# Attention queries of 15 batches by seven block products instead of eight, in a graph network kernel

## Chip, core and metric

One core of a Trainium2 chip runs the whole kernel; everything is f32. The metric is the device time of one launch in microseconds. Engines: PE is TensorE (matrix products), DVE is VectorE, ACT is ScalarE, POOL is GpSimd, SP is SyncE, which issues the DMAs.

## The reference

Two layers work on x of 16 batches x 1024 nodes x 256 features. The first (graph aggregation, two dense layers with batch norms, residual, layer norm) is not touched by the change. The second is, per batch:

```
c_adj = mean(fea, axis=1)                       # fea = x transposed: 256 x 1024
A     = abs(abs(sigmoid(c_adj[n] - c_adj[m]) - 0.5) - 0.5) * 2
Wg    = adj * (A + A.T) / 2                     # gate, 1024 x 1024
g     = relu((fea @ Wg) * para)                 # queries, 256 x 1024
k, v  = split(x @ kv_w)
out   = softmax(q k^T * scale) v                # 4 heads of 64
x     = layernorm(x + out)
```

The product `fea @ Wg` is the one that the change does otherwise.

## The kernel before

The first layer runs until about 870 us of the span. It already does its large products by seven block products (`seven`, L104). The attention of all batches follows in `fast()` (L571), and there the order of all instructions is written out by hand: `tc.manual_schedule()` keeps the program order, and each engine works its queue in that order.

**Steps.** A batch is 16 steps. A step (L1188 to L1197) multiplies a block of keys with half a batch's queries for one pair of heads (`scores`, L780, matmul at L787, two PSUM buffers `ps_s`), takes the exponential (`exps`, L796, ACT at L799, six buffers `ep`), adds the exponentials up for the denominators (`sums`, L801, DVE at L805 and L808) and multiplies them with the values (`attend`, L815, PE at L823). Scores and exponentials run one step ahead. After four steps ACT copies one half of the output (L834) and DVE adds the other (L835).

**Pieces.** All other work of neighbouring batches is cut into pieces and put into slots, eight a batch (`put`, L961, from L967 on). Two slots of pieces are issued, then four steps: this is called a window here, four to a batch, numbered 0 to 3. `arrange` (L1052) orders the pieces of a slot. While batch b-1 has its steps, the pieces make batch b ready and begin batch b+1:

- `gate` (L723): ACT makes a 128x1024 block of the gate (`wg_a`, L705: L710, or L712 and L713), DVE finishes the block two before and multiplies it with adj (`wg_b`, L715: L719, L720). Eight blocks in slots 0 to 2 (`WG`, L964), each a tile of its own.
- `keys` (L731) and `values` (L741): PE at L736 and L747, copied out of PSUM by ACT; in slots 0 to 2 (`KV`).
- `graph` (L756): the product for the queries, 32 pieces of one matmul (L761), h over the two halves of the nodes, c over the two halves of the features, k over 8 blocks of 128 nodes, in slots 2 to 7 (`QG`). After each k = 7, `queries` (L767) multiplies with para (L769) and takes the relu with the scale (L770), both on DVE.
- `rows` (L616), `ln1_a` (L625) and `ln1_b` (L641): rows of batch b+1. DVE transposes and adds (L618, L619) and takes statistics (L562, L563), POOL makes scale and shift (L66, L68, L636), ACT normalises in place with a sum of each row (L646). `bn2_q` (L610) has scaled them before on POOL (L614).
- `put_x1`, `get_x1`, `x1_v` (L654 to L669): the transposed x by way of DRAM. `means` (L678) and `crow` (L683): the column means that the gate needs.
- `dens`, `fetch_o`, `finish_a`, `finish_b` (L846 to L925): denominators and the output's layer norm for the batch before.

All of these take PSUM tiles from `ps_t` (four buffers of one bank), and so does the output of `attend`, two tiles for four steps.

## Times and profile before

| | |
|---|---|
| median of 3 runs | 2460.53 us (2458.66 to 2460.64) |
| the profiled execution | 2461.81 us, its span 2460.1 us |
| granted PE clock | 0.993 |
| first score of the attention | 871.0 us into the span |
| one batch of attention, steady | 100.5 us |
| PE, DVE, ACT, POOL busy in such a batch | 100.4, 83.3, 59.0, 32.7 us |

The profiled execution is one run of its own; its span goes from the first instruction to the last. A row of a group reads: line, engine, operation, output<-inputs, shape, count, then busy time and mean ns of one, then idle time of the engine ahead of them and what ended it. A row of a timeline reads: start, duration, engine, line, operation, output<-inputs, count, and in brackets the idle time before and what ended it. In a table by stretches each engine has its busy time and its number of instructions. An f32 matmul appears as two records.

### The profile page before, as it was taken

Reading aid. Unit: us, or ns where it says so; the run is one execution under the profiler, and the core shown is the slowest. Engines: PE = TensorE matmul, PEld = TensorE weight load, DVE = VectorE, ACT = ScalarE, POOL = GpSimd, SP = SyncE. Lnnn points to the kernel's source line nnn. Section 1 sums busy time; section 2 is a strip of 40 time slices with the busy share of each in tenths; the row PEclk is TensorE's granted clock in tenths of the full one; section 3 lists DMA queues with packets and bytes.
Section 4 is the critical chain, followed back from the end, with each engine's and each line's share of the span. In section 5 each row is a group of like instructions: output and inputs, shape, how many; then the busy total and the mean of one; then the engine's idle time right before and its main releaser. Section 6 shows DMA issues by size and latency. Waiting matters only on the chain. (4 is left out here: it accounts for less than half of the span.)

```text
span 2460.1 us, 33873 instructions
## 1 busy us (share of the span) xinstructions
PE 2412.8 (98%) x12217; PEld 1009.9 (41%) x12217; DVE 1810.3 (74%) x2583; ACT 1094.1 (44%) x1549; POOL 777.2 (32%) x826
## 2 busy tenths in 40 slices
PE   8999999999899899999999999999999999999997
PEld 4444444444344443443434434344344343443432
DVE  5555545546766777888788888888888888888676
ACT  2000000001554455564655656656566465564644
POOL 2223222231566531414224143232342422414012
PEclk9999999999999999999999999999999999999998
DMA  4122122222578543544545535545364454554221
GB/s 137 68 86 103 69 86 103 82 87 88 192 278 277 133 121 84 142 122 114 141 105 124 148 89 149 120 119 148 82 150 111 119 147 96 139 128 110 68 42 52
DMA packets 583951, 292.73 MB, mean 119 GB/s; under 512 B 407528, under 2 KB 556512, under 8 KB 576608
## 3 DMA queue, kind: packets, MB, share of 16 engines
q1 hardware_dynamic: 583776, 290.49, 43.3%
q8 instruction: 98, 1.61, 0.3%
q14 instruction: 77, 0.63, 0.1%
HBM read 194.46 MB, written 95.94 MB: 118 GB/s over the span
## 5 line engine op out<-in xcount | busy, mean ns | idle before, releaser
L799 ACT ACTIVATE e<-s 128x1024 f32<-128x1024 f32 x512 | 495.8, 1020 | 327.8 <-PE s L787 264.7
L808 DVE TENSOR_TENSOR acc<-acc,e 128x1024 f32<-128x1024 f32 x384 | 508.5, 1324 | 113.3 <-ACT e L799 87.1
L787 PE MATMUL s<-qT,kT 64*64 64x512 f32 x4096 | 490.6, 594 | 4.5 <-ACT e L799 1.7
L823 PE MATMUL o<-e,v 64*64 64x512 f32 x4096 | 485.3, 589 | 0.0
L761 PE MATMUL pg<-wg,x 128*128 128x512 f32 x960 | 426.5, 597 | 0.0
L614 POOL TENSOR_TENSOR yt<-yt,stq 128x512 f32<-128x512 f32 x120 | 178.1, 1485 | 414.9 <-DMA yt<-yT 232.0
L761 PEld LDWEIGHTS pg<-wg,x 128*128 128x128 f32 x960 | 178.7, 190 | 238.6 <-issue 237.8
L823 PEld LDWEIGHTS o<-e,v 64*64 64x64 f32 x4096 | 156.6, 133 | 282.8 <-issue 275.1
L787 PEld LDWEIGHTS s<-qT,kT 64*64 64x64 f32 x4096 | 147.2, 133 | 298.4 <-issue 254.1
L107 ACT COPY u<-pa 128x512 f32<-128x512 f32 x15 | 8.8, 585 | 475.3 <-PE pa L312 475.3
L66 POOL TENSOR_SCALAR rs_z<-mv_z 128x2 f32<-128x2 f32 x64 | 18.2, 285 | 470.1 <-DVE mv_z L563 469.2
L720 DVE SCALAR_TENSOR_TENSOR wg<-wg,adj 128x1024 f32<-128x1024 f32 x128 | 163.4, 1308 | 2.8
L312 PE MATMUL pa<-AhT,x 128*128 128x512 f32 x360 | 161.8, 592 | 0.0
L646 ACT ACTIVATE x<-x,nm_a,rs_a 128x256 f32<-128x256 f32 x128 | 75.9, 594 | 171.5 <-POOL nm_a L636 171.1
L835 DVE TENSOR_TENSOR ot<-o,ot 128x512 f32<-128x512 f32 x64 | 44.2, 691 | 130.6 <-ACT ot L834 130.6
L747 PE MATMUL pv<-kvw,x1T 128*128 128x256 f32 x512 | 118.2, 384 | 0.0
L736 PE MATMUL pk<-x1T,kvw 128*128 128x512 f32 x256 | 117.9, 604 | 0.0
L343 PE MATMUL ph<-agg,SW 128*128 128x512 f32 x240 | 112.8, 592 | 0.0
L66 POOL TENSOR_SCALAR rs_a<-mv_a 128x2 f32<-128x2 f32 x64 | 38.0, 594 | 234.0 <-DVE mv_a L563 232.8
L747 PEld LDWEIGHTS pv<-kvw,x1T 128*128 128x128 f32 x512 | 96.7, 191 | 31.7 <-issue 16.2
L312 PE MATMUL pa<-T,sx 128*128 128x512 f32 x240 | 107.9, 592 | 0.0
L312 PEld LDWEIGHTS pa<-AhT,x 128*128 128x128 f32 x360 | 68.4, 190 | 86.1 <-issue 86.1
(193 smaller groups left out, 3155.2 us busy)
## 6 DMA issues: line engine op xcount, KB each, us to landing
adj<-in_adj_dram SPq DMA_DIRECT2D x128, 512.0 KB
h<-hT SPq DMA_DIRECT2D x28, 1024.0 KB
hL<-h SPq DMA_DIRECT2D x28, 1024.0 KB
ob<-o SPq DMA_DIRECT2D x248, 72.0 KB
x<-in_x_dram SPq DMA_DIRECT2D x16, 1024.0 KB
yT<-y SPq DMA_DIRECT2D x64, 256.0 KB
out_dram<-r SPq DMA_DIRECT2D x64, 256.0 KB
xr<-in_x_dram SPq DMA_DIRECT2D x62, 256.0 KB
```

The costliest lines, as they stand in the source:

```text
L312: nc.tensor.matmul(p, xs[n][:, k, :], bs[n][:, k, :], start=(k == 0), stop=(k == KN - 1))
L343: nc.tensor.matmul(p, ws[n][:, ts(f, P)], bs[n], start=True, stop=True)
L614: nc.gpsimd.tensor_tensor(y, y, sc, op)
L646: nc.scalar.activation(r, r, AF.Identity, bias=nm[:, a : a + 1], scale=rs[:, a : a + 1], accum_out=css[b][:, i : i + 1])
L720: nc.vector.scalar_tensor_tensor(t, t, 1.0, adjs[b * NT + i], op0=OP.add, op1=OP.mult)
L736: nc.tensor.matmul(p, kvw[:, k, ts(c, P)], x1Ts[b][:, k, ts(h, FB)], start=(k == 0), stop=(k == CT - 1))
L747: nc.tensor.matmul(p[:, ts(a, C)], x1Ts[b][:, k, ts(j + a, P)], kvw[:, k, C:], start=(k == 0), stop=(k == CT - 1),)
L761: nc.tensor.matmul(pg[b], x1s[b, k // 2][:, k % 2, ts(c, P)], wgs[b, k][:, ts(h, FB)], start=(k == 0), stop=(k == NT - 1))
L787: nc.tensor.matmul(t[r * HD : (r + 1) * HD, h, :], kTs[b, pair][h * HD : (h + 1) * HD, ts(2 * cb + r, HD)], qTs[b, pair, hf][h * HD : (h + ...
L799: nc.scalar.activation(E[g, a], S.pop((g, a)), AF.Exp)
L808: nc.vector.tensor_add(ACC[b, hf, pair], ACC[b, hf, pair], E[g, a])
L823: nc.tensor.matmul(O[b, hf, pair][r][h * HD : (h + 1) * HD, :], vs[b][r * HD : (r + 1) * HD, cb, pair * P + h * HD : pair * P + (h + 1) * HD],
```

## The change

It is made for batches 1 to 15, the pieces of which run during the 15 batches before; batch 0 keeps its eight products.

With x split into blocks x_ci (c half of the features, i half of the nodes) and the gate into b_ih, the four quarters of the product come from seven products of blocks, each 4 matmuls long. The sums of gate blocks are made in place, in `wgs` (one tile for the batch now), by four `sums_w` of 128x2048 on DVE; the sums of x blocks by `sums_x` on POOL, 10 instructions of 128x256, into a new tile. Products 1, 6, 7 and 4 are added onto each other in one PSUM bank (`ps_q`, taken from `ps_t`, which keeps three), which is copied by ACT after 1, 6 and 7; product 3 is added onto product 5 in another. `collect` makes the quarters on DVE: one reads PSUM alone and multiplies with para, three add PSUM to a copy first. The relu with the scale goes to ACT. The values' last two pieces move from slot 2 to slots 4 and 5, and x1T is allocated at the first `x1_v`.

```diff
-        wgp = pool("wgp", NT)
+        wgp = pool("wgp", 1)
...
-        qp = pool("qp", 2 * CT + 1)
+        qp = pool("qp", 2 * CT + 2)
+        sxp = pool("sxp", 1)
...
-        ps_t = pool("ps_t", 4, space=PSUM)
+        ps_t = pool("ps_t", 3, space=PSUM)
+        ps_q = pool("ps_q", 1, space=PSUM)
...
+        def sums_x(b, k):
+            if k == 0:
+                SX[b] = sxp.tile([P, 2, KN, P], F32, tag="sx", name=f"sx{b}")
+            for j in range(KN // 2):
+                p, q = (SX[b][:, n, 2 * j : 2 * j + 2, :] for n in range(2))
+                x00, x01, x10, x11 = (block_x(b, c, i, j) for c in range(2) for i in range(2))
+                if k == 0:
+                    nc.gpsimd.tensor_add(p, x10, x11)
+                    nc.gpsimd.tensor_sub(p, p, x00)
+                    nc.gpsimd.tensor_sub(q, x00, x10)
+                else:
+                    nc.gpsimd.tensor_add(q, x10, x11)
+                    nc.gpsimd.tensor_sub(p, x01, p)
+
+        def sums_w(b, n):
+            (b00, b01), (b10, b11) = ([block_w(b, i, h) for h in range(NH)] for i in range(2))
+            if n == 3:
+                nc.vector.tensor_sub(b01, b11, b01)
+            elif n == 2:
+                nc.vector.tensor_add(b00, b00, b01)
+            elif n == 4:
+                nc.vector.tensor_sub(b10, b10, b00)
+            else:
+                nc.vector.tensor_sub(b01, b11, b00)
...
+        def product(b, n):
+            c, i = {2: (0, 1), 4: (1, 1)}.get(n, (0, 0))
+            w = {1: (0, 0), 2: (1, 0), 3: (1, 1), 4: (1, 0), 5: (0, 1), 6: (0, 0), 7: (0, 1)}[n]
+            bank = {1: 0, 6: 0, 7: 0, 4: 0, 2: 1, 5: 2, 3: 2}[n]
+            if n in (1, 2, 5):
+                PB[b, bank] = (ps_t if bank else ps_q).tile([P, FB], F32, tag="t", name=f"pg{bank}")
+            for k in range(KN):
+                x_ = block_x(b, c, i, k // 2)[:, k % 2, :] if n in (1, 2, 4) else SX[b][:, n in (7, 5), k, :]
+                nc.tensor.matmul(
...
+                    start=(k == 0 and n in (1, 2, 5)),
+                    stop=(k == KN - 1),
...
+            if n == 1:
+                t = queries_tile(b, 0, 0)
+                queries_tile(b, 1, 0)
+                nc.scalar.copy(t, PB[b, 0])
+            if n in (6, 7):
+                nc.scalar.copy(queries_tile(b, n - 6, 1), PB[b, 0])
+
+        def collect(b, c, h):
+
+            t, p = qTs[b, c, h], PB[b, {(0, 0): 1, (1, 0): 0}.get((c, h), 2)]
+            if (c, h) != (1, 0):
+                nc.vector.tensor_add(t, p, t)
+                p = t
+            nc.vector.tensor_mul(t, p, para_sb[:, c, ts(h, FB)])
+
+        def relu(b, c, h):
+            nc.scalar.activation(qTs[b, c, h], qTs[b, c, h], AF.Relu, scale=scale)
...
-        KV = (2, 3, 3)
-        QG = (4, 6, 5, 5, 6, 6)
+        KV = (2, 3, 1)
...
+            for t, f, *a in (
+                (2, sums_x, 0),
+                (3, product, 1),
+                (3, sums_w, 3),
+                (3, sums_w, 2),
+                (4, product, 2),
+                (4, values, 4),
+                (4, product, 6),
+                (5, collect, 0, 0),
+                (5, values, 6),
+                (5, product, 7),
+                (5, sums_w, 4),
+                (5, sums_x, 1),
+                (5, sums_w, 1),
+                (6, product, 5),
+                (6, relu, 0, 0),
+                (6, product, 4),
+                (7, collect, 1, 1),
+                (7, product, 3),
+                (7, collect, 1, 0),
+                (7, collect, 0, 1),
+                (NC, relu, 1, 0),
+                (NC + 1, relu, 0, 1),
+                (NC + 1, relu, 1, 1),
+            ):
+                put(b - 1, t, f, b, *a)
...
+            return -1 if f is collect and a[1:] == (1, 1) else rank.get(f, len(rank))
...
+            return f in (sums_w, sums_x) or f is collect and a[1:] == (0, 1)
...
-            return first + order + [fa for fa in alone if fa[0] is crow]
+            return first + order + end + [fa for fa in alone if fa[0] is crow]
```

By the last lines, `collect` (1, 1) goes ahead of a slot's other short pieces, and `sums_w`, `sums_x` and `collect` (0, 1) behind all of them. In a slot the order of the others stays as it was: in slot 3, for one, `rows`, `ln1_a` and `ln1_b` of the batch after next come ahead of product 1, and in slot 6 `finish_a`, `x1_v` and `means` ahead of what slot 7 holds.

More of the change, by code (lines that the diff above doesn't have):

```diff
@@ L619, in rows, with x1T_tile @@
             nc.vector.tensor_add(x1s[b, j], x1s[b, j], xrs[b, j])
+        def x1T_tile(b):
+            x1Ts[b] = x1Tp.tile([P, CT, N], F32, tag="x1T", name=f"x1T_{b}")
         def begin(b):
-            x1Ts[b] = x1Tp.tile([P, CT, N], F32, tag="x1T", name=f"x1T_{b}")
+            if b < 2:
+                x1T_tile(b)
             css[b] = sm.tile([P, NT], F32, tag="cs", bufs=2, name=f"cs_{b}")
@@ L668, in x1_v @@
         def x1_v(b, j):
+            if j == 0:
+                x1T_tile(b)
             nc.vector.transpose(x1Ts[b][:, :, ts(j, 2 * P)], XB.pop((b, j)).rearrange("p (c n) -> p c n", c=CT))
@@ L705, in wg_a @@
         def wg_a(b, i):
-            t = wgp.tile([P, N], F32, tag="wg", name=f"wg_{b}_{i}")
-            wgs[b, i] = t
+            if i == 0:
+                wgs[b] = wgp.tile([P, NT, N], F32, tag="wg", name=f"wg_{b}")
+            t = wgs[b][:, i, :]
             if i < SIGNED:
@@ L715, in wg_b @@
         def wg_b(b, i):
-            t = wgs[b, i]
+            t = wgs[b][:, i, :]
             if i < SIGNED:
@@ L754, in values @@
             nc.scalar.copy(vs[b][:, j : j + 2, :], p.rearrange("p (a c) -> p a c", a=2))
-        def graph(b, m):
-            h, c, k = m // (CT * NT), m // NT % CT, m % NT
-            if k == 0:
-                pg[b] = ps_t.tile([P, FB], F32, tag="t", name="pg")
-            nc.tensor.matmul(
-                pg[b], x1s[b, k // 2][:, k % 2, ts(c, P)], wgs[b, k][:, ts(h, FB)], start=(k == 0), stop=(k == NT - 1)
-            )
-            if k == NT - 1:
-                queries(b, c, h, pg[b])
+        SX, PB = {}, {}
@@ new lines, in fast, with block_w, block_x @@
+        KN = NT // 2
+        def block_w(b, i, h):
+            return wgs[b][:, i * KN : (i + 1) * KN, ts(h, FB)]
+        def block_x(b, c, i, j):
+            return x1s[b, i * KN // 2 + j][:, :, ts(c, P)]
+        def sums_x(b, k):
+            if k == 0:
+                SX[b] = sxp.tile([P, 2, KN, P], F32, tag="sx", name=f"sx{b}")
[9 more added lines that the diff above has]
+                    nc.gpsimd.tensor_sub(p, x01, p)
@@ new lines, in sums_w, with queries_tile @@
+        def sums_w(b, n):
[8 more added lines that the diff above has]
+                nc.vector.tensor_sub(b01, b11, b00)
+        def queries_tile(b, c, h):
+            qTs[b, c, h] = qp.tile([P, FB], F32, tag="qT", name=f"qT_{b}_{c}_{h}")
+            return qTs[b, c, h]
@@ new lines, in product @@
+        def product(b, n):
[7 more added lines that the diff above has]
+                nc.tensor.matmul(
+                    PB[b, bank],
+                    x_,
+                    block_w(b, *w)[:, k, :],
+                    start=(k == 0 and n in (1, 2, 5)),
+                    stop=(k == KN - 1),
+                    skip_group_check=n in (3, 4, 6, 7),
+                )
+            if n == 1:
[4 more added lines that the diff above has]
+                nc.scalar.copy(queries_tile(b, n - 6, 1), PB[b, 0])
@@ L767, in queries @@
+        def collect(b, c, h):
[6 more added lines that the diff above has]
+            nc.scalar.activation(qTs[b, c, h], qTs[b, c, h], AF.Relu, scale=scale)
         def queries(b, c, h, p):
-            qs = qTs[b, c, h] = qp.tile([P, FB], F32, tag="qT", name=f"qT_{b}_{c}_{h}")
+            qs = queries_tile(b, c, h)
@@ L1021, in fast @@
                     put(b - 1, t, f, *a)
-            m = 0
-            for t, n in enumerate(QG):
-                for m in range(m, m + n):
-                    put(b - 1, NC - len(QG) + t, graph, b, m)
-                m += 1
+            for t, f, *a in (
[24 more added lines that the diff above has]
+                put(b - 1, t, f, b, *a)
         put(B - 1, 4, range_so_far)
@@ L1030, in fast, with rank_of, is_last @@
         nsteps = B * NS
-        order = (dens, recips, x1_t, finish_a, fetch_o, finish_b, x1_v, rows, ln1_a, ln1_b, put_x1, get_x1, means, load, crow)
+        order = (dens, recips, x1_t, finish_a, fetch_o, finish_b, relu, x1_v, rows, ln1_a, collect, ln1_b, put_x1, get_x1, means, load, crow)
         rank = {f: k for k, f in enumerate(order)}
+        def rank_of(fa):
+            f, a = fa
+            return -1 if f is collect and a[1:] == (1, 1) else rank.get(f, len(rank))
+        def is_last(fa):
+            f, a = fa
+            return f in (sums_w, sums_x) or f is collect and a[1:] == (0, 1)
         short = (dens, recips, x1_t, back)
@@ L1039, in is_short @@
             return f in short
-        long = (keys, values, graph)
+        long = (keys, values, product)
         def spread(few, many):
@@ L1057, in arrange @@
             alone = [fa for fa in pieces if fa[0] in (dens, back, recips, crow)]
-            few = [fa for fa in pieces if fa not in first + gates + many + alone]
-            few.sort(key=lambda fa: rank.get(fa[0], len(rank)))
+            end = [fa for fa in pieces if is_last(fa)]
+            few = [fa for fa in pieces if fa not in first + gates + many + alone + end]
+            few.sort(key=rank_of)
             few_pe = [fa for fa in few if is_short(fa)]
@@ L1069, in arrange @@
                     for k, o in enumerate(order):
-                        if o[0] in rank and rank[o[0]] <= rank.get(fa[0], len(rank)):
+                        if o[0] in rank and rank_of(o) <= rank_of(fa):
                             at_ = k + 1
                     order.insert(at_, fa)
-            if any(fa[0] is graph for fa in many):
+            if len(many) < 2:
                 order = gates + order
@@ L1104, in graph0 @@
                         x1s[0, k // 2][:, k % 2, ts(c, P)],
-                        wgs[0, k][:, ts(h, FB)],
+                        wgs[0][:, k, ts(h, FB)],
                         start=(k == 0),
```

## Prediction

> **What bounds the kernel now.** I read the engine totals first, then one batch of the attention stage cut into its four windows (a window is two slots of pieces and then four attention steps; windows 0 to 3 below), then the order of instructions in the windows that the change touches.

> ```profile
> PE 2412.8 (98%) x12217; PEld 1009.9 (41%) x12217; DVE 1810.3 (74%) x2583; ACT 1094.1 (44%) x1549; POOL 777.2 (32%) x826
> ...
> L761 PE MATMUL pg<-wg,x 128*128 128x512 f32 x960 | 426.5, 597 | 0.0
> ```

> PE is never without work, and the query product (L761) is 426.5 us of it. An f32 matmul leaves two records: 15 batches x 32 matmuls = 480 make 960.

> ```profile
> core 0: us, PE busy (x) PEld busy (x) DVE busy (x) ACT busy (x) POOL busy (x), PEclk, DMA share, GB/s
> 1475.80:1500.10 24.30, 24.17 (x164) 9.15 (x160) 20.29 (x18) 18.63 (x22) 6.70 (x4) 1.00 0.69 168
> 1500.10:1528.00 27.90, 27.90 (x177) 13.09 (x173) 21.56 (x27) 17.22 (x24) 12.36 (x12) 1.00 0.54 151
> 1528.00:1551.90 23.90, 23.90 (x161) 8.62 (x157) 21.88 (x38) 11.38 (x18) 9.48 (x16) 1.00 0.44 84
> 1551.90:1576.30 24.40, 24.40 (x157) 9.32 (x153) 19.54 (x32) 11.73 (x18) 4.11 (x8) 1.00 0.34 87
> ```

> The four rows are windows 0 to 3 of one batch: 100.5 us, PE full in each, and DVE second with 83.3 us. So each microsecond taken from PE counts, but only as long as nothing else in that window takes nearly as long. In window 1 something does (timelines of PE, DVE, POOL and ACT):

> ```profile
> 1500.14 5.45 PE L747 MATMUL pv<-kvw,x1T 128*128 128x256 f32 x24
> 1505.42 8.75 PE L761 MATMUL pg<-wg,x 128*128 128x512 f32 x20
> 1514.10 1.95 PE L787 MATMUL s<-qT,kT 64*64 64x512 f32 x16
> ```

> ```profile
> 1500.86 0.69 DVE L835 TENSOR_TENSOR ot<-o,ot 128x512 f32<-128x512 f32 x1 [2.07 <-ACT ot L834]
> ...
> 1503.32 4.63 DVE L720 SCALAR_TENSOR_TENSOR wg<-wg,adj 128x1024 f32<-128x1024 f32 x4
> ...
> 1510.32 0.18 DVE L563 BATCH_NORM_AGGREGATE mv_a<-st_a 128x2 f32<-128x6 f32 x1
> ```

> ```profile
> 1510.67 0.22 POOL L66 TENSOR_SCALAR rs_a<-mv_a 128x2 f32<-128x2 f32 x1 [12.96 <-DVE mv_a L563]
> ...
> 1511.79 0.54 POOL L636 TENSOR_SCALAR nm_a<-mv_a,rs_a 128x1 f32<-128x1 f32 x2
> ```

> ```profile
> 1512.13 0.60 ACT L646 ACTIVATE x<-x,nm_a,rs_a 128x256 f32<-128x256 f32 x1 [3.63 <-POOL nm_a L636]
> ...
> 1513.22 0.19 ACT L646 ACTIVATION_READ_ACCUMULATOR x<-x,nm_a,rs_a 128x1 f32 x1
> 1515.25 1.02 ACT L799 ACTIVATE e<-s 128x1024 f32<-128x1024 f32 x1 [1.84 <-PE s L787]
> ```

> This is a chain: DVE adds up the last window's output, multiplies four gate rows (L720), makes the statistics of the batch after next; POOL turns them into scale and shift; ACT's normalisation (`ln1_b`, L646) waits for these 3.63 us; and this window's first new exponential (L799) stands behind it in ACT's queue. The chain is free at 1513.4, 1.84 us before PE's scores let the exponential go. PE's graph matmuls are what covers it. I measured the start of that L646 in windows of all batches: 11.9 us after the window's start in 14 of 15; the last has none, since no batch is left to normalise.

> [...]mean record 597 ns, yet window 3's 24 run from 1551.86 to 1562.26, 0.433 us apart; I use 0.433. [...]the trace's copies of 512 are 0.58, and the relu with two pointers (L478) 0.80. [...]

> ```profile
> L268 DVE TENSOR_TENSOR T<-AhT x1: 2291/2291/2291, 54.0 to 54.0; 128x2048 f32<-128x2048 f32 x1
> L269 DVE TENSOR_TENSOR T<-AhT,T x1: 3236/3236/3236, 56.3 to 56.3; 128x2048 f32<-128x2048 f32 x1
> ```

> The same 2048-element sum takes 2.29 us alone and 3.24 beside POOL's sums.

> **The change, part by part.** All of it is per batch from the second on, in the 15 windows-of-four before each.

> *PE, total.* Seven products of 4 matmuls instead of 32: 4 matmuls, 8 records x 0.433 = 3.47 us less, 52 us in all. By window: window 1 had 20 records of graph and 24 of values (0.22 each), and keeps 8 of product 1 and 8 of values: -12 x 0.433 - 16 x 0.22 = -8.7. Window 2 had 20 of graph and gets 24 of products 2, 6, 7 and 16 of values: +5.25. Window 3 has 24 either way. Window 0 is as before.

> *Window 1.* PE's values (1.76), product 1 (3.47), one step's scores (1.77) and its attend (1.71) end 8.7 us after the start, at 1508.8. The next scores need a score buffer that the first new exponential frees, and that stands behind `ln1_b` (free at 1513.4) and the new copy of product 1 (0.5): it runs 1513.9 to 1514.9, and PE goes on at 1515.05. Before, these scores began at 1517.58. So the window shrinks by 2.5 us, not 8.7: 6.2 us of new stall. Nothing of the chain is moved by the change: the two value copies that ACT loses stood in its waiting time; POOL's six sums of half 0 stand behind nm_a.

> *VectorE.* Four in-place sums of 2048 elements (2.29 to 3.24, I take 2.5: 10 us), three sums with PSUM (0.69 each, as L835), less four relus (L770, 0.44): +10.3 us, 93.6 of a batch. The sums stand last in their slots, ahead of the steps' accumulations. In window 1 two of them (5 us, from 1513.1) put the first accumulation's end at about 1521, and the exponential that needs its buffer comes at 1522.7: no stall. In window 2 DVE runs through, starting about 1.6 us late after window 1, and ends its last accumulation some 0.8 us behind PE; the exponential in question has 2 us in hand.

> *Window 3.* Product 3 adds onto product 5's bank, so it waits until `collect` (1,1) has read that. In DVE's queue that stands behind the output sum, an accumulation, a `finish_a`, a transpose and the means. In the trace these end 7.0 us after the window's start in all 14; with the read (0.69) it is 7.7, and with the 0.8 of lag less what the ACT copy hides, 8.2. PE arrives after products 5 and 4, 6.9. Stall 1.3; bounds 0.8 (no lag) to 4 (3 us more DVE contention). DVE's later queue, finish and collects, has until the third step.

> *Window 0.* ACT gets three relus[...]. The first falls into ACT's 1.19 us wait for keys, the second pair into 0.49 of waiting: 0.4 to 0.8 remains ahead of the first exponential, which already holds PE by 0.3 us there (next scores at 1489.62, attend's end 1489.3). +0.45.

> *New waits.* `sums_w` 2 waits for product 1 (PE done at 1505.4, DVE there at 1515) and `sums_w` 1 for product 7, 5 us before DVE comes to it; behind them queue the accumulations, counted above. POOL's `sums_x` 1 waits for product 7 too; behind it stands window 3's finish, before which POOL idles 11.5 us now. The relu of (0,0) precedes window 3's `ln1_b` by 0.5 us; the means on DVE come 4 us after that.

> *Covered.* POOL's ten sums of 256 (0.73 each as L326, 7.3 us): POOL is 32% busy, and waits 5 us for DVE in window 2; what they cost is DVE contention, in the bounds. The copies of products 6 and 7: 1.1 us of ACT in window 2, where it idles 7.8; values stand between product 6 and 7, so the copy is done in time. One PSUM buffer fewer in the rotation: window 2's pieces are freed by ACT copies in under 1 us. No DMA is added. x1T's later allocation puts no one behind it: its values are read a window before.

> **Sum.** -2.5 + 5.25 + 1.3 + 0.45 = +4.5 us a batch, for 14 batches 63 us. The 15th has no `ln1_b`: -3.47 + 0.8 + 0.6 = -2.1. So +61 on the profiled execution's 2461.8 (span 2460.1): 2522.7. The median of the runs is 1.3 lower: 2521.5, said as 2522.

> **Rivals.**
> 1. *PE's saving arrives in full* (faster). If ACT's exponentials do not stand behind `ln1_b` as the trace has it, or the gate rows ahead of it shorten, window 1 loses 8.7: 52 us less, plus 15 x 1.75 for windows 0 and 3: 2434. It decides where the first exponential of window 1 is done by 10.5 us after the start (stall 1.7, which with 1.75 eats 3.47), not 14.9. For it: PE is the bound on the page. Against: the 3.63 us wait is in the same place in 14 batches, and queue order is the code's order throughout. 11%.
> 2. *VectorE becomes the bound.* 83.3 + 10.3 + 3 of contention is 96.6 of PE's 97.1. If sums beside POOL take 3.24, window 2 ends with DVE 3 to 4 us late, product 3 waits 4 and more: +3 to 4 a batch, 2565 to 2580. For it: window 1 needs some 27 us of DVE in 25. Against: window 0 leaves it 4 us to catch up. 15%.
> 3. *A PSUM wait in window 2*: values 6 in the bank of product 2, which its `collect` frees only behind a second finish, 6 us later: 2610. Against: no piece waits so now, with banks held across windows. 4%.

> **Numbers.** Main case 70% (2505 to 2545). The range 2500 to 2572 takes in its bounds and most of rival 2. A measurement of this kernel can tell about 0.2% from no change. Faster 0.11, within 0.2% 0.02, slower 0.87.

> **What would show it.** In the changed profile: window 1 of some 25 us with a PE gap of about 6 us ended by L799; ACT's L646 wait still there; graph matmuls down to 840 records; window 2 near 29 us without a gap; a gap of 1 to 2 before product 3 ended by DVE. I am wrong if window 1's scores go on before L646 has run, if batches take under 100.5 us, or if the gaps of PE lie elsewhere.

## The result and the profile after

The changed kernel takes 2594.34 us (median of four runs, 2590.0 to 2595.99), the kernel before 2459.8 beside it: ratio 1.0545 [1.0526, 1.0563]. The prediction was 2522, with 2572 as its upper end: the sign is right, the loss is twice as large as forecast. The profiled execution took 2590.0 us, its span is 2588.1, and its granted PE clock is 0.970 where it was 0.993.

The engine totals of the changed kernel:

```profile
PE 2413.2 (93%) x12097; PEld 996.5 (39%) x12097; DVE 2006.1 (78%) x2628; ACT 1152.6 (45%) x1654; POOL 1034.8 (40%) x976
```

PE has 120 matmul records fewer and is busy for as long as before, in a longer span: part of its work runs slower. DVE has 196 us more. One batch by windows (the columns are those of the prediction's table; this batch is one of the longer ones):

```profile
core 0: us, PE busy (x) PEld busy (x) DVE busy (x) ACT busy (x) POOL busy (x), PEclk, DMA share, GB/s
1417.17:1441.91 24.74, 24.16 (x161) 9.17 (x161) 20.42 (x18) 20.09 (x25) 6.61 (x4) 1.00 0.69 166
1441.91:1468.48 26.57, 20.87 (x146) 7.86 (x145) 25.04 (x26) 16.75 (x23) 15.69 (x12) 0.94 0.57 159
1468.48:1497.52 29.04, 29.04 (x179) 12.43 (x177) 27.87 (x39) 13.82 (x22) 23.08 (x27) 1.00 0.36 69
1497.52:1528.75 31.23, 27.69 (x155) 10.38 (x154) 24.19 (x36) 12.25 (x19) 4.13 (x9) 0.89 0.27 68
```

Windows 1 and 3 show two things that before had nowhere in a batch: PE is not full, and PEclk, the clock that it is granted, is below 1. DVE is busy for 97.5 us of the batch instead of 83.3, and in window 2 for 27.87 of 29.04. POOL has 49.5 instead of 32.7.

The table holds the means of batches 1 to 13, worked out from the traces, for all kernels of this document. "To product 3" is the time from the start of window 1 to product 3's first matmul, and here the median of these batches. "Half clock" is the time in which PE was granted half its clock. "DVE waits" are DVE's gaps of more than 0.25 us, as far as they lie in windows 1 to 3; smaller ones, between its instructions, make another 3.2 to 3.9 us a batch.

| kernel | us | window 0 | 1 | 2 | 3 | batch | to product 3 | PE idle | half clock | DVE waits |
|---|---|---|---|---|---|---|---|---|---|---|
| before | 2459.8 | 24.30 | 27.86 | 23.87 | 24.50 | 100.5 | | 0.1 | 0 | 9.8 |
| predicted | 2522 | 24.75 | 25.4 | 29.1 | 25.8 | 105.0 | 62.7 | 7.5 | | |
| changed | 2594.3 | 24.74 | 26.91 | 29.04 | 29.80 | 110.5 | 66.2 | 9.4 | 9.7 | 5.7 |
| e1 | 2598.1 | 24.74 | 25.29 | 29.04 | 31.62 | 110.7 | 66.2 | 5.9 | 5.0 | 5.9 |
| e2 | 2576.3 | 24.74 | 25.29 | 29.04 | 29.51 | 108.6 | 66.2 | 2.5 | 0 | 3.8 |
| e3 | 2529.9 | 24.75 | 26.66 | 29.04 | 25.38 | 105.8 | 63.4 | 6.9 | 3.4 | 4.7 |
| e4 (of before) | 2430.4 | 24.30 | 26.29 | 23.87 | 24.50 | 99.0 | | 3.3 | 3.4 | 9.1 |
| e5 | 2575.9 | 24.75 | 19.36 | 36.92 | 28.28 | 109.3 | 66.3 | 8.0 | 6.8 | 4.5 |
| e6 | 2530.7 | 24.74 | 27.33 | 29.04 | 24.65 | 105.8 | 63.3 | 6.4 | 6.8 | 1.0 |
| e7 | 2529.7 | 24.75 | 19.36 | 36.75 | 24.89 | 105.8 | 63.0 | 5.4 | 6.6 | 0.9 |
| e8 | 2473.8 | 24.30 | 20.98 | 31.69 | 24.88 | 101.9 | 59.4 | 3.2 | 1.6 | 0.3 |
| e9 | 2530.5 | 24.74 | 25.29 | 29.04 | 26.55 | 105.6 | 61.7 | 2.8 | 0 | 0.9 |
| e10 | 2475.8 | 23.95 | 20.98 | 32.71 | 24.78 | 102.4 | 60.3 | 3.5 | 1.8 | 0.4 |
| e11 | 2472.4 | 24.30 | 20.98 | 32.13 | 24.50 | 101.9 | 60.2 | 2.8 | 2.1 | 2.0 |
| e12 | 2475.0 | 23.95 | 20.98 | 31.47 | 25.94 | 102.3 | 59.1 | 3.6 | 1.6 | 0.2 |
| e13 | 2400.8 | 23.95 | 20.98 | 27.11 | 24.50 | 96.5 | 55.0 | 0 | 0 | 4.0 |
| e14 | 2505.4 | 24.80 | 27.06 | 28.05 | 24.50 | 104.4 | 62.3 | 3.8 | 5.3 | 7.3 |
| e15 (of before) | 2482.9 | 25.16 | 27.86 | 24.73 | 24.50 | 102.3 | | 0.1 | 0 | 14.9 |
| e16 | 2434.2 | 24.81 | 20.98 | 28.31 | 24.81 | 98.9 | 56.3 | 0.1 | 0 | 2.1 |

The thirteen batches account for the loss: 13 x 9.96 = 129.5 us, against 128.2 between the two profiled executions (the last batch gains 2.9).

**Window 1** of the changed kernel, which starts at 1441.84 here; a timeline of ACT and PE:

```profile
1448.97 1.90 PE L898 MATMUL o<-e,v 64*64 64x512 f32 x16
1453.85 0.60 ACT L652 ACTIVATE x<-x,nm_a,rs_a 128x256 f32<-128x256 f32 x1 [4.60 <-POOL nm_a L642]
...
1455.03 0.56 ACT L827 COPY qT<-pg 128x512 f32<-128x512 f32 x1
1455.49 1.93 ACT L874 ACTIVATE e<-s 128x1024 f32<-128x1024 f32 x2
1456.56 3.34 PE L862 MATMUL s<-qT,kT 64*64 64x512 f32 x16 [5.70 <-ACT e L874]
```

This is the queue that the prediction followed: `ln1_b` (now L652) waits for POOL, the copy of product 1 and the first new exponential stand behind it, and PE waits 5.70 us. The last line shows what it did not have: the sixteen scores take 3.34 us after the gap, where sixteen matmuls of the same size took 1.90 ahead of it.

**Window 3**, which starts at 1497.45; timelines of DVE and PE:

```profile
1491.82 9.37 DVE L883 TENSOR_TENSOR acc<-acc,e 128x1024 f32<-128x1024 f32 x6
1501.11 0.69 DVE L910 TENSOR_TENSOR ot<-o,ot 128x512 f32<-128x512 f32 x1
...
1507.38 0.69 DVE L835 TENSOR_TENSOR qT<-pg,qT 128x512 f32<-128x512 f32 x1
```

```profile
1497.45 3.70 PE L816 MATMUL pg<-wg,sx 128*128 128x512 f32 x8
...
1508.13 6.62 PE L816 MATMUL pg<-wg,sx 128*128 128x512 f32 x8 [3.54 <-DVE qT L835]
```

DVE ends window 2's accumulations at 1501.1, 3.7 us after PE is through with that window, and so the read that product 3 waits for (`collect` (1,1), L835) comes 10.6 us after the window's start. Product 3's eight records take 6.62 us behind the gap, product 5's took 3.70.

The waits of the whole kernel (us in total, times, longest):

```profile
PE s L862 <- ACT e L874: 90.2, 29, 6.5
```

and the groups concerned:

```profile
L883 DVE TENSOR_TENSOR acc<-acc,e 128x1024 f32<-128x1024 f32 x384 | 545.0, 1419 | 87.0 <-ACT e L874 56.2
L816 PE MATMUL pg<-wg,sx 128*128 128x512 f32 x480 | 244.3, 657 | 40.6 <-DVE qT L835 40.6
```

The products of summed blocks take 657 ns a record and the scores 618, where plain products still take 597 and the scores took 594; the accumulation on DVE takes 1419 ns where it took 1324.

### The profile page after: what moved, and what is told of

It is laid out like the page before. It is cut to its first block, busy times and chain, and to the rows that moved or that the text cites. A ratio compares the mean times of both kernels' runs of the same rounds, so it can differ in the third digit from the quotient of the medians.

```text
span 2588.1 us, 33885 instructions
## 1 busy us (share of the span) xinstructions
PE 2413.2 (93%) x12097; PEld 996.5 (39%) x12097; DVE 2006.1 (78%) x2628; ACT 1152.6 (45%) x1654; POOL 1034.8 (40%) x976
## 5 line engine op out<-in xcount | busy, mean ns | idle before, releaser
L883 DVE TENSOR_TENSOR acc<-acc,e 128x1024 f32<-128x1024 f32 x384 | 545.0, 1419 | 87.0 <-ACT e L874 56.2
L862 PE MATMUL s<-qT,kT 64*64 64x512 f32 x4096 | 512.9, 618 | 91.1 <-ACT e L874 90.2
L616 POOL TENSOR_TENSOR yt<-yt,stq 128x512 f32<-128x512 f32 x120 | 187.1, 1560 | 412.9 <-DMA yt<-yT 207.3
L816 PE MATMUL pg<-wg,sx 128*128 128x512 f32 x480 | 244.3, 657 | 40.6 <-DVE qT L835 40.6
L816 PE MATMUL pg<-wg,x 128*128 128x512 f32 x360 | 163.4, 597 | 0.0
L816 PEld LDWEIGHTS pg<-wg,sx 128*128 128x128 f32 x480 | 98.4, 211 | 167.5 <-issue 100.9
L66 POOL TENSOR_SCALAR rs_z<-mv_z 128x2 f32<-128x2 f32 x64 | 18.9, 295 | 350.2 <-DVE mv_z L563 349.1
L652 ACT ACTIVATE x<-x,nm_a,rs_a 128x256 f32<-128x256 f32 x128 | 75.9, 593 | 141.9 <-POOL nm_a L642 141.3
L66 POOL TENSOR_SCALAR rs_a<-mv_a 128x2 f32<-128x2 f32 x64 | 36.4, 569 | 223.0 <-DVE mv_a L563 221.6
L756 PE MATMUL pv<-kvw,x1T 128*128 128x256 f32 x512 | 124.7, 388 | 0.0
L642 POOL TENSOR_SCALAR nm_a<-mv_a,rs_a 128x1 f32<-128x1 f32 x128 | 120.4, 955 | 6.3
L756 PEld LDWEIGHTS pv<-kvw,x1T 128*128 128x128 f32 x512 | 95.8, 192 | 49.6 <-issue 29.8
```

Of the source, the lines that this page charges most:

```text
L616: nc.gpsimd.tensor_tensor(y, y, sc, op)
L642: nc.gpsimd.tensor_scalar(nm[:, a : a + 1], mv[:, a, 0:1], rs[:, a : a + 1], -1.0, op0=OP.mult, op1=OP.mult)
L756: nc.tensor.matmul(p[:, ts(a, C)], x1Ts[b][:, k, ts(j + a, P)], kvw[:, k, C:], start=(k == 0), stop=(k == CT - 1),)
L816: nc.tensor.matmul(PB[b, bank], x_, block_w(b, *w)[:, k, :], start=(k == 0 and n in (1, 2, 5)), stop=(k == KN - 1), skip_group_check=n in ...
L862: nc.tensor.matmul(t[r * HD : (r + 1) * HD, h, :], kTs[b, pair][h * HD : (h + 1) * HD, ts(2 * cb + r, HD)], qTs[b, pair, hf][h * HD : (h + ...
L883: nc.vector.tensor_add(ACC[b, hf, pair], ACC[b, hf, pair], E[g, a])
```

## The experiments

**First theories.** A: what was missed is the clock; after a gap PE runs at half of it for some us, in both windows. B: DVE runs without a break from window 1 to the read of product 3, so that its work sets the batch, and PE's gaps only show it.

**e1 and e2** fill PE's gaps with unused matmuls, so that the clock has no gap to fall in: six in window 1 (e1), and four more in window 3 (e2).

```diff
+        def dummy(b, n):
+            p = ps_t.tile([P, FB], F32, tag="t", name="dum")
+            for k in range(n):
+                nc.tensor.matmul(p, block_x(b, 0, 0, 0)[:, 0, :], block_w(b, 1, 1)[:, 0, :], start=True, stop=True)
...
                 (3, product, 1),
+                (3, dummy, 6),
...
                 (6, product, 4),
+                (6, dummy, 4),
```

> The changed kernel with six matmuls of 128x512 more per batch on PE, their result unused, behind product 1 in window 1 (5.2 us of PE work at full clock, in the place of the 5.7 us gap). Theory (the gap lets PE's granted clock fall to half for 3.4 to 6.8 us, and that costs time of its own): window 1 has no half-clock stretch any more, is 25 us long instead of 26.9, and the kernel gets 1.9 us x 14 = 27 us faster, though PE does 78 us more work; some 2568. Rival (the halved clock costs nothing, since PE would wait for others anyway): same time as the changed kernel, 2594, or up to 20 us slower.

> As the run before, with four more such matmuls behind product 4 in window 3 (3.5 us, in the place of its 3.1 us gap). Theory of the clock: no half-clock stretch in either window, granted clock back near 0.99, window 3 at 27.5 to 28 us instead of 29.8, together 4.2 us a batch less: 2594 - 59 = 2535. Rival (clock without effect): 2594 or more.

e1: 2598.1 us, ratio 1.0561 [1.0544, 1.0579]. The half clock leaves window 1, which shrinks by 1.6 us, and the batch is as long as before the edit: window 3's gap grows from 3.1 to 4.7. The time to product 3 stays at 66.2 to the tenth. e2: 2576.3, 1.0472 [1.0454, 1.0489]: no half clock is left, and with 9 us more of PE's work a batch the kernel is 18 us faster than the change. The step from e1 to e2 is window 3's half clock: product 3 starts as late as before, and the window is 2.1 us shorter. So it lies on the path, and that of window 1 does not. e1 came out as its rival had it; e2 lies between its two forecasts. Most of the loss is neither half clock.

**e3** leaves out the ten block sums on POOL; **e4** is the kernel before with less of PE's work in window 1.

```diff
         def sums_x(b, k):
-            if k == 0:
-                SX[b] = sxp.tile([P, 2, KN, P], F32, tag="sx", name=f"sx{b}")
+            if not SX:
+                t = sxp.tile([P, 2, KN, P], F32, tag="sx", name="sx")
+                nc.gpsimd.memset(t, 0.0)
+                SX.update({b_: t for b_ in range(B)})
+            return
```

> The changed kernel without the ten sums of x blocks on GpSimd per batch: the products that use them read zeros, so the queries are other numbers. Theory (VectorE's lag behind window 2 is contention with these sums): the accumulations go back from 1.45 to some 1.33 us, VectorE's busy time per batch falls from 97.3 to 93 us, the gap ahead of product 3 from 3.1 to 1.3 us, and the half-clock stretches in window 3 mostly vanish; window 1 keeps its gap of 5.7. Time 2594 - 14 x (1.8 + 2.2) = 2538. Rival (the lag is the four in-place sums alone): the gap stays at 3 and the time above 2585.

> The kernel before with eight of the ten graph matmuls of window 1 left out in each of 15 batches (6.9 us of PE work a batch, 104 us in all), nothing else changed; part of the query sums is missing. Theory (window 1 has a floor that the normalisation in ACT's queue sets): PE's work is lost to a gap of about 4 us ended by the exponential; the window shrinks by 3 us, less about 1 to 2 for half clock after the gap: 2460 - 14 x 1.5 - 7 = 2432, between 2415 and 2445. Rival (PE bounds the window): 2356.

e3: 2529.9 us (one run), 64 less than the change, for 7.3 us of POOL work by the prediction's price. The time to product 3 falls to 63.4, the gap in window 3 to 0.6, and the half clock there is gone. DVE, which has the same instructions as in the change, is busy for 93.6 us of a batch instead of 97.3. This is contention of POOL and DVE, and the trace of the change shows it directly. Window 1 again, DVE and then POOL:

```profile
1454.80 2.26 DVE L796 TENSOR_TENSOR wg<-wg 128x2048 f32<-128x2048 f32 x1
1457.17 2.63 DVE L798 TENSOR_TENSOR wg<-wg 128x2048 f32<-128x2048 f32 x1
1459.72 10.73 DVE L883 TENSOR_TENSOR acc<-acc,e 128x1024 f32<-128x1024 f32 x6
```

```profile
1454.81 2.84 POOL L787 TENSOR_TENSOR sx<-sx,x 128x256 f32<-128x256 f32 x1
```

A block sum takes 2.84 us beside a gate sum, and six accumulations take 10.73 us, 1.79 each. I sorted all 384 accumulations of the change by what POOL did during them: 1.225 us where POOL did nothing (176 of them), 1.215 where it did only its small operations on one or two columns, 1.66 where it worked on `sx` or `yt` for 95% of the time or more (112). Not every instruction of DVE was slower beside POOL: L116, a sum of the first layer of which one input lies in PSUM (`hT<-ph,v`), takes 0.683 us beside POOL's sums (28 times) and 0.683 without (twice), and statistics (L562 on `x`) take 0.40 in both cases.

The two engines don't lose alike. Beside a gate sum it is POOL that stands still: in 14 batches a block sum that begins with L796 ends 0.59 us behind it, and L796 takes 2.26 us, no more than such a sum alone (2.29). An operation of POOL on one column (L642) mostly takes 2.37 or 3.36 us there, 0.27 alone. Beside the accumulations both are slower: DVE by 0.43 us each, and POOL's block sums take some 1.7 us instead of 0.73.

e4: 2430.4 us (one run), 29 less than before for 104 us of PE's work. That is the floor that the prediction drew for window 1: 8 of 10 graph matmuls less a batch in that window give 1.6 us; the rest turns into a gap of 3.1 us, ended by the same exponential, and 3.41 us at half clock behind it.

**e5** takes `ln1_b` out of the way of window 1's exponential; **e6** puts the read of product 3 first in DVE's queue; **e7** does both.

```diff
-                    put(b - 2, j + 3, ln1_b, b, j)
-                    put(b - 2, j + 3, put_x1, b, j)
+                    put(b - 2, max(j + 3, 4), ln1_b, b, j)
+                    put(b - 2, max(j + 3, 4), put_x1, b, j)
```

```diff
-                (7, collect, 1, 1),
+                (6, collect, 1, 1),
...
+            lead = [fa for fa in order if fa[0] is collect and fa[1][1:] == (1, 1)]
+            if lead:
+                lead = [fa for fa in order if fa[0] is product and fa[1][1] == 5] + lead
+                order = lead + [fa for fa in order if fa not in lead]
```

> The changed kernel with one normalisation (ln1_b and put_x1 of the batch's first two row blocks) moved from slot 3 to slot 4, so that nothing that waits for GpSimd stands ahead of window 1's exponentials. Theory A (window 1's gap is a cost of its own, as the prediction had it): the gap of 5.7 us goes, with its half clock, and nothing takes its place: 2594 - 14 x 7.3 = 2490. Theory B (VectorE works without a break from window 1's start to the read that product 3 waits for, 66.1 us, and that sets the time): the gap of window 1 goes, but PE waits as long elsewhere, 5 us ahead of the denominators in window 2 for the accumulations, or ahead of product 3; product 3 starts again 66 us after window 1's start, a batch stays at 109 to 111 us, 2575 to 2600.

> The changed kernel with collect (1,1) directly behind product 5 in the order, ahead of one finish_a, one transpose and the means on VectorE. Theory B: VectorE's 66.1 us ahead of product 3 become 61.4, PE comes at 62.8, so the gap of window 3 goes with its half clock (3.1 + 2.2 us) and the gap of window 1 stays: a batch of 104.9, 2594 - 14 x 5.5 = 2517. Theory A (the gap of window 1 with its half clock is the bound, that of window 3 a small one): no more than 1.3 us a batch, 2576.

> Both edits together. Theory B: VectorE's way to product 3 is 61.4 us, so a batch takes 24.7 + 61.4 + 17.3 = 103.4 us and some half clock behind a gap at the denominators in window 2: 2500 to 2520, hardly better than the early collect alone. Theory A: both gaps and all half clock go, 97.6 us a batch, 2594 - 14 x 12.9 = 2413.

e5: 2575.9, 1.047 [1.0452, 1.0487]. Window 1's gap is gone (19.36 us), and the time to product 3 is 66.3 as before: PE now waits for DVE in window 2, ahead of the denominators, which need the accumulations:

```profile
1459.86 10.72 DVE L883 TENSOR_TENSOR acc<-acc,e 128x1024 f32<-128x1024 f32 x6
...
1470.64 1.92 PE L927 MATMUL pd<-acc,ones 128*32 128x512 f32 x4 [4.60 <-DVE acc L883]
```

Theory A is dead as the main cause, B stands: 5.7 us of stall were taken away and given back in window 2. That e5 is 18 us faster than the change comes from window 3, which has 1.6 us of half clock a batch instead of 4.5. e6: 2530.7, 1.029 [1.0273, 1.0307], 64 us from one place in a queue; the gap in window 3 falls to 0.04 and DVE waits some 1 us in windows 1 to 3 together. e7: 2529.7 (one run), no more than e6: the stall of window 1 is worth nothing while DVE is full. Both are slower than theory B had them (2517, and 2500 to 2520), and far from theory A (2576 and 2413).

**e9** asks whether e6 is held by the half clock in its window 1 (6.8 us of it a batch) or by DVE: e6 and the six unused matmuls of e1.

> As e6 (collect (1,1) right behind product 5), and six unused 128x512 matmuls (5.2 us of PE) behind product 1 in window 1. In e6 VectorE's path was out of the way, and every batch spent 6.8 us at half clock in window 1 (27.3 us long). Theory: there the clock lies on the path; with no long gap there is no half clock, window 1 takes 25.3 as in e1, 14 x 2.0 = 28 less than e6 although PE does 73 us more work: 2503 (2495 to 2512). Rival: what the half clock costs lies beside VectorE's work; then the time is that of e6, 2528 to 2535, as e1's was that of the changed kernel.

2530.5, 1.0286 [1.0268, 1.0303]: the rival's number. Window 1 is 2.0 us shorter, as forecast, and window 3 is 1.9 longer, mostly by a wait of PE for DVE's `means` (1.5 us). Where PE would wait for DVE further on in any case, half of its clock costs nothing; behind the last such wait it does cost, as the step from e1 to e2 showed.

**e8, e10, e12** try to make the change pay by order alone. e8 is e7 with one `finish_a` between window 0's steps, the denominators of half 0 a slot later, the values' third piece two slots sooner, two relus a slot later and the gates first in their slot. e10 is e8 with POOL's first block sums a slot sooner (the gates now come first in that slot, and no longer in the one behind it); e12 is e10 with `collect` (0,0) a slot sooner and first on DVE, and the denominators behind product 7.

```diff
-        KV = (2, 3, 1)
+        KV = (2, 3, 2)
...
-                put(b, t, dens, b, hf)
+                put(b, t + (hf == 0 and b < B - 1), dens, b, hf)
...
+                    if hf == 1 and k == 0 and b < B - 2:
+                        between[(b + 1) * NS + 2] = [(finish_a, (b, j))]
+                        t_a = None
...
-                (2, sums_x, 0),
+                (1, sums_x, 0),
...
-                (5, collect, 0, 0),
+                (4, collect, 0, 0),
```

> Both edits, and VectorE's work moved out of windows 1 and 2: one finish_a into the steps of window 0, where VectorE is idle for 4 us; the denominators from slot 4 to slot 5; one values piece back into slot 2; two relus from slot 1 to slot 2. Theory B: VectorE's way to product 3 is 57.7 us against PE's 55.4, a batch of 99.7 to 101: 2445 to 2465, about the kernel before. Theory A: 97 us, 2405.

> As e8, and POOL's first six block sums start in window 0 (slot 1), in which POOL waits 13 us, instead of window 1 (slot 2). In e8 they ran until 4 us into window 2 and held up scale and shift of ln1_b there: the copy of product 6 stood behind ln1_b in ACT's queue, PE waited 1.5 us for it ahead of product 7, 1.1 us for VectorE ahead of the denominators, and the half clock followed. Theory (POOL's sums cost by where they stand in the queue, as much as by their contention): one of these gaps goes, window 2 shrinks by 1 to 2 us, 2450 to 2462. Rival (VectorE's total, 96.1 us of a batch, is what counts; the contention only moves to window 0): 2470 to 2480.

> As e10, with two places in window 2 changed: collect (0,0) right behind product 2, in slot 4 instead of slot 5 (in e10 and e11 it stood on VectorE behind two transposes, their statistics and a finish_a, and an attend waited 2 us for it), and the denominators behind product 7 instead of ahead of it (PE waited 2 us there for VectorE's output sum). No work is added or left out. In e11 VectorE's busy time fell by 1.8 us a batch and the time did not move: that the load as a whole is the bound there has fallen. Theory now (what PE waits for is the place of the reads in VectorE's queue): both gaps go, 3.4 us, and most of 1.8 us of half clock with them: 98 to 99.5 a batch, 2420 to 2442, faster than before. Rival (VectorE has 30 us of work to do in window 2 and the wait reappears at its next read): 2465 to 2480.

e8: 2473.8, 1.0053 [1.0037, 1.007]; e10: 2475.8, 1.0068 [1.0052, 1.0085]; e12: 2475.0, 1.006 [1.0047, 1.0074]. e8 is just slower than the kernel before, 9 us above the range of theory B, and e10 and e12 gain nothing on it: both came out as their rivals had it. In e10 the gap of 1.5 us ahead of product 7 went as forecast, but the denominators' grew from 1.1 to 1.9, and in 8 of 13 batches one of 2 us came at an attend. e12 took both away, and 2.4 us came back a little later in window 2, and in most batches 1.4 in window 3. The one in window 2, in a timeline of all engines:

```profile
1438.99 0.18 DVE L563 BATCH_NORM_AGGREGATE mv_a<-st_a 128x2 f32<-128x6 f32 x1
...
1439.27 0.22 POOL L66 TENSOR_SCALAR rs_a<-mv_a 128x2 f32<-128x2 f32 x1 [8.31 <-DVE mv_a L563]
...
1441.01 0.60 ACT L652 ACTIVATE x<-x,nm_a,rs_a 128x256 f32<-128x256 f32 x1 [8.70 <-POOL nm_a L642]
...
1442.34 0.56 ACT L763 COPY v<-pv 128x512 f32<-128x512 f32 x1
...
1442.95 1.93 PE L898 MATMUL o<-e,v 64*64 64x512 f32 x12 [2.39 <-ACT v L763]
```

PE waits for a copy of the values on ACT, which stands behind `ln1_b`, which waits for POOL, and POOL for statistics late in DVE's queue. Windows 2 and 3 of this batch:

```profile
core 0: us, PE busy (x) PEld busy (x) DVE busy (x) ACT busy (x) POOL busy (x), PEclk, DMA share, GB/s
...
1424.62:1455.44 30.82, 28.43 (x169) 10.92 (x169) 29.45 (x37) 15.82 (x27) 19.69 (x19) 1.00 0.40 82
1455.44:1481.84 26.40, 24.93 (x154) 9.23 (x154) 25.00 (x36) 12.26 (x19) 6.46 (x11) 1.00 0.36 87
```

DVE is busy for 29.45 of 30.82 and 25.00 of 26.40; the rest is some 40 ns behind each of its instructions.

**e11** is e8 without POOL's block sums, as e3 was to the change.

> As e8, and POOL's ten block sums are left out (products 6, 7, 5 and 3 read zeros in their place, so the queries are not those of the reference; all of PE's, VectorE's and ACT's instructions are as in e8). In e8 and e10 VectorE is without a wait of over 0.25 us for all but 1.7 us of a batch of 101.9, so theory (VectorE's work is the bound there, 3.7 us of it from the contention with POOL's sums, as e3 showed against the changed kernel): 3 to 3.7 us less a batch, 98.2 to 99: 2425 to 2440, faster than before. Rival (the waits of PE in window 2 are the order of the queues, not VectorE's load): 2465 to 2480.

2472.4 (one run): the rival's number, and a forecast of mine that fell. DVE's busy time fell by 1.8 us a batch, but all of that and more in window 3 (23.4 to 21.4); in windows 1 and 2 it rose from 50.8 to 51.1, since POOL, rid of the sums, scaled the rows (L616) beside the accumulations at window 2's start instead (in each batch two of them took 2.07 and 2.03 us). This left open whether DVE's load or the order of the other queues held window 2.

**e13** settles that: e12 without DVE's four gate sums, all queues else as they were.

```diff
         def sums_w(b, n):
+            return
```

> As e12, and VectorE's four in-place gate sums (9.3 us a batch) are left out, so that the products multiply the gate's blocks as they are and the queries are not those of the reference; POOL's block sums and all the rest stay. In e12 VectorE has no wait of over 0.25 us in windows 1, 2 and 3 of any batch, while PE waits 2.4 us in window 2 and 1.1 in window 3, so theory (VectorE's load sets the batch, and every wait of PE that an order takes away comes back at VectorE's next read): without the sums PE is the bound, 96.4 to 98 us a batch as in the last batch of e12 (96.9), 2390 to 2415, well below the kernel before. Rival (the queues of ACT and POOL in window 2 hold PE up whatever VectorE has to do): 98 to 101 us less what little moves, 2440 to 2470.

2400.8 us, ratio 0.976 [0.9732, 0.9788]. Its totals and windows 2 and 3:

```profile
PE 2354.9 (98%) x12097; PEld 1016.3 (42%) x12097; DVE 1863.7 (78%) x2568; ACT 1147.8 (48%) x1654; POOL 1044.9 (44%) x976
```

```profile
1400.53:1427.64 27.11, 27.11 (x169) 10.95 (x169) 24.23 (x33) 14.19 (x25) 18.84 (x20) 1.00 0.48 97
1427.64:1452.14 24.50, 24.50 (x154) 9.36 (x154) 20.71 (x33) 12.25 (x19) 2.88 (x8) 1.00 0.35 88
```

PE is full in every batch, none is at half clock, and the batch takes 96.5 us, 4.0 less than before. In e12 no product waited for a gate sum itself, so what went is their time in DVE's queue. So this is what seven products are worth on PE once their operands cost nothing on DVE; the in-place sums (9.5 us of a batch) cost 74 us of time between e12 and e13.

**e14, e15, e16** take work from DVE without leaving any of the result out: the last exponential of each chain isn't added on DVE, but on PE in the denominators' product, four accumulations less a batch. e14 (on e12) has five e tiles in rotation and one apart, e16 six and one apart and three buffers for gate rows instead of four. e15 is the same edit as e14, on the kernel before.

```diff
                 for a in range(2):
-                    nc.vector.tensor_add(ACC[b, hf, pair], ACC[b, hf, pair], E[g, a])
+                    if not held(cp, a):
+                        nc.vector.tensor_add(ACC[b, hf, pair], ACC[b, hf, pair], E[g, a])
...
-            for pair in range(NP):
-                acc = ACC.pop((b, hf, pair))
-                for h in range(2):
-                    k = 32 * (2 * pair + h)
-                    nc.tensor.matmul(p[k : k + 32, :], ones32, acc[:, h, :], start=True, stop=True)
+            for n, part in enumerate((ACC, EH)):
+                for pair in range(NP):
+                    acc = part.pop((b, hf, pair))
+                    for h in range(2):
+                        k = 32 * (2 * pair + h)
+                        nc.tensor.matmul(
+                            p[k : k + 32, :], ones32, acc[:, h, :], start=n == 0, stop=n == 1, skip_group_check=True
+                        )
```

> As e12, with four of VectorE's 24 accumulations of a batch taken away: the last e tile of each chain isn't added to acc (L883), and the denominators add it up on PE instead, by four more matmuls of 32 columns behind the four that a half has (the four take 1.06 us together, so an estimated 0.9 more a half). The result is the same. The e tiles are five in rotation and one set apart, where they were six. Theory (VectorE's load sets the batch, as e13 showed by leaving out its gate sums): VectorE loses 4 x 1.44 = 5.8 us of 101.2, PE gains 1.8 on 96.5, the batch takes 98 to 99.5: 2420 to 2445, faster than the kernel before. Rival (an e buffer fewer makes ACT wait for VectorE, or the denominators wait longer than they save): 2465 to 2490.

> The kernel before, with the same edit of the accumulations and the denominators as in e14 and nothing else. Theory (PE is the bound there, VectorE isn't): nothing gained, 1.8 us of PE more a batch, 2470 to 2490. Rival (four accumulations fewer help that kernel as well): 2430 to 2455.

> As e14, with six e tiles in rotation again beside the one set apart, and a gate row buffer fewer (adjp three instead of four) to make room. In e14 windows 0, 2 and 3 took 24.8, 28.0 and 24.5 us without a gap of PE, but in window 1 an exponential waited 3.5 to 4.2 us for an e tile that VectorE's accumulation had not freed, and the half clock followed. Theory (VectorE's load was the bound of e12, the e tile was e14's own new wait): window 1 goes back to 20.98 as in e12 and e13, 98.3 a batch, 2425 to 2440, faster than the kernel before. Rival (VectorE is late in window 1 whatever the buffers, or the gates now wait for their rows): 2470 to 2505.

e14: 2505.4, 1.019 [1.0176, 1.0204], slower than e12 and above both forecasts: windows 2 and 3 got shorter, but in window 1 ACT waits for an e tile, as the rival had it:

```profile
1855.12 1.02 ACT L883 ACTIVATE e<-s 128x1024 f32<-128x1024 f32 x1 [4.72 <-DVE acc L893]
1856.20 1.91 PE L862 MATMUL s<-qT,kT 64*64 64x512 f32 x8 [3.45 <-ACT e L883]
```

e16, with that tile back: **2434.2 us, ratio 0.9894 [0.9878, 0.9911]**, 1.1% faster than the kernel before and 6% faster than the change.

```profile
PE 2387.1 (98%) x12353; PEld 1022.7 (42%) x12353; DVE 1928.2 (79%) x2564; ACT 1144.7 (47%) x1654; POOL 1089.7 (45%) x976
```

DVE has 82 us less than in e12 and PE no gap. e15: 2482.9, 1.0091 [1.0076, 1.0107]: on the kernel before, the same edit costs 1.7 us a batch, all of it in windows 0 and 2, where the denominators are. There PE was the bound, and the lighter DVE gained nothing. So the gain belongs to the change, with its new order, and the edit together. The kernel before in the new order was not run; its PE idles for 0.1 us a batch, so there is little for an order to win.

## Why the prediction was wrong, step by step

**Right.** Window 0 (24.75 forecast, 24.74 measured; the time of its three relus on ACT was the author's estimate; a relu, L840, took 0.62 us), window 2 (29.1 and 29.04), and in window 1 the queue with its times: the first new exponential 13.9 to 14.9 us after the start (13.7 to 14.7), the gap 6.2 us (5.7). The gate sums cost 9.5 us, forecast 10. The last batch, without `ln1_b`, gains 2.9, forecast 2.1. PE's records fell to 840.

**Failed: the step "VectorE".** It had DVE end window 2's accumulations "some 0.8 us behind PE", and the stall ahead of product 3 at 1.3. In the batch shown it is 3.7 us behind, and the read comes 10.6 us after window 3's start instead of 8.2. The term that was mis-sized is contention, which stood under "Covered" and in the bounds only. POOL's ten sums take 1.6 to 2.8 us each where they meet DVE's two-input sums, not 0.73, POOL's busy time grew by 16.9 us and not by 7.3, and they stretch the accumulations from 1.23 to 1.66. A price taken from a stretch in which POOL was alone was used for one in which DVE never rests. And the forecast looked for DVE's loss in the gate sums (2.29 to 3.24 each), where POOL is the one that loses; it fell on the accumulations, 1419 ns instead of 1324 in the mean, 2.3 us a batch. On the path it is 66.2 instead of 62.7 us to product 3, 3.5 a batch or 46 us over 13; e3 gives back 2.8 of them, and the other 0.7 was not traced.

**Failed: the gaps' own price.** The sum counted a gap of PE at its length and had no term for the clock. In nearly every batch the half clock followed: in the mean 5.25 us in window 1 and 4.46 in window 3, and in window 3, on the path, half of 4.46 is 2.2 us. From product 3 to the end of window 3 the forecast has 17.6 us and the trace 19.6. With the 3.5 above that is 5.5 a batch, the whole difference between 105.0 and 110.5. The stall ahead of product 3, 3.1 us in the mean, still lies in the bounds that the prediction gave it, 0.8 to 4; the clock is what no bound held.

**Failed in its reading: window 1's stall as a cost.** The working adds the four windows' gains and losses. They don't add: e5 and e7 show that window 1's 5.7 us can go without a microsecond gained from it, since DVE needs windows 1 and 2 whole. A stall of PE there was the place where the bound showed, not the bound. So the sign came out right for another reason than the sum gives: DVE's path to product 3 makes the batch longer, with that stall or without it.

**Of the rivals,** the second had the mechanism: DVE as the bound, because of sums beside POOL, deciding at product 3. Its 2565 to 2580 lacked the half clock (2576.3 was measured in e2, where that is filled away, though with 9 us more of PE's work). What spoke against it, that "window 0 leaves it 4 us to catch up", was no help: the read of product 3 comes before window 0. The first (2434, PE's saving in full) is what e13 shows once the places of the waits are mended and DVE's gate sums are gone: 2400.8, more than it claimed. The third did not occur: no piece waits for a PSUM buffer.

**Left open.** Contention was not split by source: e3 and e11 took POOL's block sums away, the row scalings (L616), which slow DVE in the kernel before as well, were always there. And no run gives PE a gap of set length and place, so what the last section says of the clock is read from traces, not tested by an edit.

## What to carry to other kernels

An engine at 83% of another's load, as DVE was here, can become the bound when a change adds work to it and takes work from the other; compare the two per stage, after the change, with contention in the price. A stall is a cost only if nothing else runs without a break past it: follow the second engine's queue through it to the next place where the first waits for it, and take that time. If removing one wait moves the time to another, count the load: here re-ordering brought the kernel from 2594 to 2474 us and no further, and four accumulations less a batch (e16) brought it to 2434.

## What the hardware showed that was not expected

```profile
core 0: us, PE busy (x) PEld busy (x) DVE busy (x) ACT busy (x) POOL busy (x), PEclk, DMA share, GB/s
1449.19:1452.60 3.41, 1.67 (x16) 0.31 (x8) 3.25 (x8) 0.05 (x1) 0.22 (x1) 1.00 0.92 284
1452.60:1456.01 3.41, 0.00 (x0) 0.00 (x0) 3.27 (x7) 2.17 (x6) 3.15 (x5) 1.00 1.01 295
1456.01:1459.43 3.42, 2.87 (x16) 1.04 (x20) 3.31 (x2) 2.23 (x3) 3.42 (x2) 0.50 0.89 233
1459.43:1462.84 3.41, 3.41 (x36) 1.11 (x32) 3.31 (x3) 1.52 (x3) 3.33 (x3) 1.00 0.90 189
```

The gap of 5.70 us covers the whole of the second step, 3.41 us, and the third is at half clock; that one has 0.55 us of idle PE, and the fourth is at full clock. What sets the steps is not shown by any run.
- **Contention by what POOL does.** Beside POOL's operations on one or two columns (L66, L68, L642) an accumulation on DVE is as fast as alone (1.215 us), beside its sums and scalings of whole tiles 1.66. The other way round even a small operation is slowed: L642 took 2.37 and 3.36 us beside gate sums of DVE.
